# Three maxima slots per item ahead of the attention, and a ScalarE copy of the denominators in layer 1

## The chip, the core and the metric

The kernel runs on one core of a Trainium2 chip. The metric is the device time of one execution in microseconds (us); for the kernel before it is the median of three runs. The core has TensorE (PE, the matmul engine), VectorE (DVE), ScalarE (ACT), GpSimd (POOL) and SyncE (SP, which here only issues transfers). Each runs its own list of instructions in order and waits on semaphores for the others. Matmul results land in PSUM, which PE writes and DVE and ACT read[...].

## What is computed

Two layers on x of shape (2, 256, 64, 64), so two batches of N = 4096 positions. Layer 0 is an attention with 8 heads of width 32, layer 1 a non-local block with a pooled softmax.

```python
# layer 0
q, k, v = split(w_qkv @ x)                      # 8 heads, d = 32, n = 4096
attn = softmax(q^T k / sqrt(d))                 # rows of 4096
x = w_proj @ (attn v) + x
# layer 1
g     = maxpool2(g_w @ x + g_b)                 # 256 x 1024
theta = theta_w @ x[:, :64] + theta_b           # 64 x 4096
phi   = maxpool2(phi_w @ x[:, 64:] + phi_b)     # 64 x 1024
y = softmax(theta^T phi) g                      # rows of 1024
x = batchnorm(W_w @ y + W_b) + x
```

Both softmaxes subtract the maximum of a row before the exponential, so each needs the maxima first, and divides by the sum of a row (the denominator) at the end.

## The kernel before

**Layer 0.** The 8 heads of a batch are two groups of four ("quads"), so there are four units of work, each with 8 blocks of 512 queries. For a block, the attention loop goes over 32 pieces of 128 keys: scores, exponentials on ACT, products with v, sums of the exponentials on POOL. The row maxima of a block have to be there before its attention starts. A generator, `maxes`, yields after each small step of the maxima, in the order of the blocks; `advance(maxes, n)` takes n steps. During the attention two steps stand in each of the 32 rounds, so that the maxima run `LEAD` = 4 rounds and one block ahead.

**Ahead of the attention** there is nothing to hide the first block's maxima, so they run next to the first projections. This front part is issued from the last lines of `conv_attention` (L840 to L853). An *item* is `make("k", 0, i)`, `make("q", 0, i)` or `make("v", 0, i)`: one projection of 512 positions, two matmuls of 128x512 for k and q, eight of 128x128 for v, into a PSUM tile of the pool `ps_m`, and an ACT copy out of it (L211, L194). The first block's maxima come from `first_block` as 33 *slots*. A slot has four matmuls, one for each head (L293), on four different groups of 32 rows of PE, so that they run beside each other. Heads 0 and 1 write into two tiles of `ps_m`, heads 2 and 3 into the two halves of one tile of `ps_s`. The maximum over a pair of key blocks a and b is found as max(b - a, 0) + a: in one slot a head has the product with the key difference, which ACT passes through Relu (L358), in its next slot the product with a itself, which DVE adds to it and reduces (`joint`, L320). Heads 2 and 3 are one slot behind heads 0 and 1, so every full slot has two Relus and two joints. In even slots the joints are those of heads 2 and 3, in odd slots those of heads 0 and 1.

**Buffers.** `ps_m` has four tiles of one bank (`scratch`), which in the front part are given out in turn; `ps_s` has two tiles of two banks (`scores`). An item takes one scratch, a slot two scratches and one scores tile. The next owner of a tile waits for the ACT or DVE instruction that read it last.

**Order of the front before:** k0, k1, q0; then k2 to k7, v0 and v1, with four slots behind each; the last slot; q1; then for each of v2 to v7 one step of the second block's maxima ahead of it (a *step* has two matmuls, for two heads, each followed by a DVE reduction at L305, or by Relu and joint); two more steps. `make_rows()` stands behind v3 and v5; its second call puts the first block's maxima through PE (L150) as rows and copies them (L161), which the attention needs.

**Layer 1.** `non_local` goes over 8 blocks i of 512 positions, in four steps t each: scores (`f2`, L805), exponentials on ACT (L820), and, one step late, `weigh`: four matmuls of 128x512 (L771) into two accumulators `acc[i]` in scratch tiles, while POOL adds the exponentials into `sums` (L763, L767). In between stands one step of `maxima1`: two matmuls (L739) into a scores tile and a DVE reduction (L746). When a block's last `weigh` is issued, `result(i)` follows: a matmul with ones gives the denominators in a scratch tile `den` (L783), DVE takes their reciprocal into `r` in SBUF (L785), two pairs of DVE instructions make z (L787, L790), and SP stores it (L793). Two of the next block's accumulators are then taken from the tiles that come free.

Of the kernel before, what the change touches and what calls it, by code (L numbers as in the profile page):

```python
# [25 lines left out]
NI = N // NB  # L26
# [9 lines left out]
def conv_attention(  # L36
# [13 lines left out]
    nc = tc.nc  # L50
# [20 lines left out]
    def scratch(name):  # L71
        return ps_m.tile([P, NB], F32, tag="m", name=name)
# [3 lines left out]
    def single(name):  # L76
        return probs.tile([P, 2, NB], F32, tag="one", name=name, bufs=ONES)
# [9 lines left out]
    def load_x(b, i, t):  # L87
        nc.sync.dma_start(
            out=t, in_=x[b].rearrange("(o p) n -> p o n", p=P)[:, :, bass.ts(i, NB)]
        )  # L90
        return t
# [76 lines left out]
    q, k, v, kd = {}, {}, {}, {}  # L168
    held = {}

    def make(what, n, i):
        b, qd = QUAD[n]
        if (b, i) not in held:
            name = f"x_{what}_{n}_{i}"
            held.clear()
            held[b, i] = load_x(b, i, xs.tile([P, NC, NB], F32, tag="x", name=name))
        xc = held[b, i]
        name = f"{what}_{b}_{qd}_{i}"
        pq = scratch(name)
        if what == "v":  # L180
            if i == 0:
                v[n] = qkv.tile([P, NJ, QH, D], F32, tag="v", name=f"v_{n}")
            for j in range(NB // P):
                for c in range(NC):
                    nc.tensor.matmul(  # L185
                        pq[:, bass.ts(j, P)],
                        xc[:, c, bass.ts(j, P)],
                        wv_sb[:, c, bass.ts(qd, P)],
                        start=(c == 0),
                        stop=(c == NC - 1),  # L190
                    )
                if j % 2 == 1:
                    yield
            nc.scalar.copy(v[n][:, bass.ts(i, NB // P)].rearrange("p j h d -> p (j h d)"), pq)  # L194
            return
        for c in range(NC):
            nc.tensor.matmul(  # L197
                pq,
                wqk_sb[:, c, qd, 0 if what == "q" else 1, :],
                xc[:, c, :],  # L200
                start=(c == 0),
                stop=(c == NC - 1),
            )
            yield
        if what == "q":
            to = q[n, i] = qkv.tile([P, NB], F32, tag="q", name=f"q_{n}_{i}", bufs=3)
        else:
            if i == 0:
                k[n] = qkv.tile([P, N], F32, tag="k", name=f"k_{n}")
            to = k[n][:, bass.ts(i, NB)]  # L210
        nc.scalar.copy(to, pq)  # L211
        if what == "k" and i % 2 == 0 and i > 0 and n == 0:
            between(n, i // 2 - 1)
        if what == "k" and i == NI - 1 and n == 0:
            rounds(n)
        if what == "k" and i % 2 == 1 and n == 0:
            if i == 1:
                kd[n] = qkv.tile([P, NI // 4, NB], F32, tag="kd", name=f"kd_{n}")
            differences(n, i // 2, (kd[n] if i < NI // 2 else last_kd)[:, i // 2 % (NI // 4), :])
# [5 lines left out]
    def differences(n, c, to):  # L225
        two = k[n][:, bass.ts(c, 2 * NB)]
        nc.gpsimd.tensor_sub(to, two[:, NB:], two[:, :NB])
# [6 lines left out]
    def between(n, c):  # L234
        two = k[n][:, NB * (2 * c + 1) : NB * (2 * c + 3)]
        nc.gpsimd.tensor_sub(mid_kd[:, c, :], two[:, NB:], two[:, :NB])

    def rounds(n):
        nc.gpsimd.tensor_sub(
            turn_kd,  # L240
            k[n][:, P:NB].rearrange("p (a n) -> p a n", n=P),
            k[n][:, N - NB : N - P].rearrange("p (a n) -> p a n", n=P),
        )
# [117 lines left out]
    G = NB // P  # L361
# [38 lines left out]
    def all_maxima():  # L400
        for n in range(len(QUAD)):
            for i in range(NI):
                yield from maxima(n, i)

    maxes = all_maxima()

    def advance(steps, n=1):
        for _ in range(n):
            next(steps, None)
# [3 lines left out]
    def make_rows():  # L413

        for i, r in enumerate(rows):
            if callable(r):
                if i in seen:
                    rows[i] = r()
                seen.add(i)
# [233 lines left out]
    def non_local(b, y, theta_w, phi_w):  # L653
# [125 lines left out]
        def result(i):  # L779
            cols = bass.ts(i, NB)  # L780
            z = single(f"z_{b}_{i}")
            den = scratch(f"den1_{b}_{i}")
            nc.tensor.matmul(den, ones, acc[i][NC], start=True, stop=True)  # L783
            r = work.tile([P, NB], F32, tag="r", name=f"r1_{b}_{i}", bufs=1)
            nc.vector.reciprocal(r, den)  # L785
            for o in range(NC):
                nc.vector.scalar_tensor_tensor(  # L787
                    z[:, o, :], acc[i][o], bn_scale[:, o : o + 1], r, ALU.mult, ALU.mult
                )
                nc.vector.scalar_tensor_tensor(  # L790
                    z[:, o, :], z[:, o, :], bn_shift[:, o : o + 1], y[:, o, cols], ALU.add, ALU.add
                )
            nc.sync.dma_start(out=dst[:, :, cols], in_=z)  # L793
# [3 lines left out]
        for i in range(NI):  # L797
            rows = later
            for t in range(last + 1):
                if t == 0:  # L800
                    s = scores(f"f2_{b}_{i}")
                for h in range(2):
                    half = bass.ts(h, CM)
                    keys = phi if t == 0 else dphi[:, 2 * P * (t - 1) :]
                    nc.tensor.matmul(  # L805
                        s[:, h, :],
                        keys[half, bass.ts(h, P)],
                        theta[i][half, :],
                        start=(t == 0),
                        stop=(t > 0),  # L810
                        skip_group_check=t > 0,
                    )
                for h in range(2):
                    half = bass.ts(h, CM)
                    if t == 0:
                        nc.tensor.matmul(
                            s[:, h, :], ones_b[half, :], rows[half, :], start=False, stop=True
                        )
                p = single(f"p1_{b}_{i}_{t}")
                nc.scalar.activation(p, s, AF.Exp)  # L820
                if waiting is not None:
                    weigh(*waiting)
                waiting = (i, t, p)
                if finish:
                    result(finish.pop())
                if t == last and i + 1 < NI:
                    later = ready[i + 1]()
                advance(maxes1)
        weigh(*waiting)
        result(finish.pop())  # L830


    LEAD = 4
# [6 lines left out]
        held[0, i] = load_x(0, i, x0[:, :, bass.ts(i, NB)])  # L840
    for what, i in (("k", 0), ("k", 1), ("q", 0)):
        advance(make(what, 0, i), 3)
    for what, i in [("k", i) for i in range(2, NI)] + [("v", 0), ("v", 1)]:
        advance(make(what, 0, i), 3)
        advance(maxes, G)
    advance(maxes)
    advance(make("q", 0, 1), 3)
    for i in range(2, NI):
        advance(maxes)
        advance(make("v", 0, i), 3)  # L850
        if i in (3, 5):
            make_rows()
    advance(maxes, 2 * LEAD - NI + 2)  # L853
    held.clear()
    for b in range(B):
        y = big.tile([P, NC, N], F32, tag="y", name=f"y{b}")
# [58 lines left out]
```

## Time and profile before

| what | us |
|---|---|
| median of three runs (3903.01 to 3907.87) | 3904.28 |
| the profiled execution | 3908.37 |
| its span, first to last instruction | 3906.6 |
| PE busy | 3864.0 |
| POOL busy | 3091.5 |
| DVE busy | 2900.7 |
| ACT busy | 2697.5 |
| front part, start of k2 to the attention's first matmul | 14.92 to 96.56 |
| layer 1, first batch, first exponential to the end of the last reciprocal | 1833.1 to 2023.1 |

Busy time of PE is pipelined and its ends are modelled, so a PE that is busy all the time may still be waiting for small amounts; how far apart the starts of equal pieces of work lie says more. PE's granted clock was 0.997 over the span. In the tables of the prediction a row of the timeline reads: start, length, engine, line, operation, what it writes and reads, and in brackets the idle time of its engine before it and what ended that. A row of the chain of waits reads: start, length, what the end of the program was waiting for at that time.

### The profile page before, as it was taken

How to read it: one execution, taken by the hardware profiler on the slowest of the kernel's cores; microseconds unless marked ns; L12 is line 12 of the kernel's file. 1: busy time of each engine (PE TensorE's matmuls, PEld its weight loads, DVE VectorE, ACT ScalarE, POOL GpSimd, SP SyncE). 2: the span in 40 equal slices, each digit the busy share in tenths (PEclk: the TensorE clock that was granted, in tenths of full speed). 3: DMA queues.
4: the chain of work that ended last, by engine and by line, in shares of the span. 5: the costliest groups of instructions: out<-in, count | busy, mean ns of one | idle time of the engine just before them, and what ended most of it. 6: DMA issues, size and time to landing. Idle time of an engine off the chain costs nothing.

```text
span 3906.6 us, 69965 instructions
## 1 busy us (share of the span) xinstructions
PE 3864.0 (99%) x27452; PEld 1366.8 (35%) x27452; DVE 2900.7 (74%) x5449; ACT 2697.5 (69%) x3378; POOL 3091.5 (79%) x1957
## 2 busy tenths in 40 slices
PE   9999999999999999999999999999999999999998
PEld 4333333333333333333333333333333333332333
DVE  5888888788888888764458888888888888884444
ACT  5787777777777777751137777777778888887111
POOL 1888899899989999871448899998999999997043
PEclk9999999999999999999999999999999999999999
DMA  1778878778878788780018888887788888889100
GB/s 57 145 167 169 172 166 170 168 162 172 168 167 169 166 168 169 167 188 6 22 34 169 168 175 168 173 171 164 163 176 171 170 170 170 168 168 188 53 17 27
DMA packets 112300, 566.26 MB, mean 145 GB/s; under 512 B 20200, under 2 KB 22504, under 8 KB 50784
## 3 DMA queue, kind: packets, MB, share of 16 engines
q0 software_dynamic: 68832, 501.25, 63.5%
q1 hardware_dynamic: 42448, 59.74, 4.5%
q8 instruction: 215, 3.52, 0.3%
q14 instruction: 117, 0.96, 0.1%
q10 hardware_dynamic: 688, 0.79, 0.1%
HBM read 51.63 MB, written 8.88 MB: 15 GB/s over the span
## 4 chain that ended last, share of the span: by engine, by line
PE 96%; DVE 2%; DMA 1%; POOL 1%; issue 0%; ACT 0%; DVEq 0%; POOLq 0%; ACTq 0%; SPq 0%
PE s L452 28%; PE w L476 26%; PE ps L293 23%; PE y L771 6%; PE q L197 2%; PE k L197 2%; PE v L185 2%; PE proj L639 1%; PE g L696 1%; DVE r L785 1%; PE f L739 1%; PE f L805 1%; PE den L536 1%; DMA p<-p 1%; PE tp L680 0%; PE tp L676 0%
## 5 line engine op out<-in xcount | busy, mean ns | idle before, releaser
L509 POOL TENSOR_TENSOR p<-p,p 128x1024 f32<-128x1024 f32 x945 | 2364.4, 2502 | 281.4 <-ACT p L598 262.7
L598 ACT ACTIVATE p<-s 128x1024 f32<-128x1024 f32 x2048 | 2087.6, 1023 | 560.5 <-PE ps L293 495.1
L293 PE MATMUL ps<-k,q 32*128 32x512 f32 x6142 | 2020.6, 626 | 2.5 <-DVE r L785 1.3
L305 DVE TENSOR_REDUCE part<-ps 128x1 f32<-128x512 f32 x2046 | 1315.7, 686 | 566.8 <-PE ps L293 563.1
L476 PE MATMUL w<-p,v 128*32 128x512 f32 x8192 | 1091.0, 605 | 1.1 <-ACT p L598 1.1
L452 PE MATMUL s<-q,mid_kd 32*128 32x512 f32 x3072 | 771.2, 615 | 0.0
L320 DVE CUSTOM_DVE_ANT_0 ps<-ps,over 128x512 f32<-128x512 f32 x1025 | 706.2, 691 | 24.9 <-PE ps L293 10.5
L491 DVE TENSOR_TENSOR y<-y,w 128x512 f32<-128x512 f32 x961 | 659.1, 686 | 51.9 <-PE w L476 49.3
L293 PEld LDWEIGHTS ps<-k,q 32*128 32x128 f32 x6142 | 625.1, 183 | 25.6 <-DVE part L320 10.4
L313 ACT ACTIVATE over<-ps 128x512 f32<-128x512 f32 x961 | 569.3, 592 | 10.7 <-PE ps L293 7.9
L293 PE MATMUL ps<-kd,q 32*128 32x512 f32 x1056 | 525.9, 593 | 0.0
L452 PE MATMUL s<-q,last_kd 32*128 32x512 f32 x2048 | 508.5, 615 | 4.5 <-ACT p L598 4.5
L452 PE MATMUL s<-q,kd 32*128 32x512 f32 x2048 | 510.5, 616 | 0.4 <-ACT p L598 0.3
L293 PE MATMUL ps<-last_kd,q 32*128 32x512 f32 x904 | 445.1, 590 | 0.0
L476 PEld LDWEIGHTS w<-p,v 128*32 128x32 f32 x8192 | 161.6, 108 | 805.3 <-DVE part L305 775.2
L452 PEld LDWEIGHTS s<-q,mid_kd 32*128 32x128 f32 x3072 | 270.4, 183 | 443.5 <-ACT over L313 253.9
L515 POOL DMA_DIRECT2D p<-p x448 | 395.3, 882 | 27.3 <-ACT p L598 27.1
L452 PEld LDWEIGHTS s<-q,kd 32*128 32x128 f32 x2048 | 174.0, 184 | 299.8 <-ACT over L313 182.7
L452 PEld LDWEIGHTS s<-q,last_kd 32*128 32x128 f32 x2048 | 172.8, 183 | 284.9 <-ACT over L313 178.5
L771 PE MATMUL y<-p,kv 128*128 128x512 f32 x512 | 240.1, 608 | 6.4 <-DVE r L785 6.4
L820 ACT ACTIVATE p<-f 128x1024 f32<-128x1024 f32 x64 | 65.5, 1023 | 248.5 <-PE f L805 219.2
L767 POOL TENSOR_TENSOR sums<-sums,p 128x512 f32<-128x512 f32 x96 | 121.3, 1264 | 113.7 <-ACT p L820 109.9
(120 smaller groups left out, 2806.3 us busy)
## 6 DMA issues: line engine op xcount, KB each, us to landing
p<-p POOLq DMA_DIRECT2D x478, 1024.0 KB, 7.6
x_q<-in_x_dram SPq DMA_DIRECT2D x30, 512.0 KB
x_k<-in_x_dram SPq DMA_DIRECT2D x24, 512.0 KB
x_res<-in_x_dram SPq DMA_DIRECT2D x16, 512.0 KB
out_dram<-z SPq DMA_DIRECT2D x16, 512.0 KB
r<-flat SPq DMA_DIRECT2D x120, 64.0 KB
x<-in_x_dram SPq DMA_DIRECT2D x8, 512.0 KB
wqk_sb<-in_wqk_dram ACTq DMA_DIRECT2D x1, 512.0 KB
```

Of the source, the lines that this page charges most:

```text
L197: nc.tensor.matmul(pq, wqk_sb[:, c, qd, 0 if what == "q" else 1, :], xc[:, c, :], start=(c == 0), stop=(c == NC - 1),)
L293: nc.tensor.matmul(ps, q[n, i][bass.ts(h, D), bass.ts(g, P)], keys[bass.ts(h, D), :], start=True, stop=True,)
L305: reduced = nc.vector.tensor_reduce(part[:, g, h, j : j + 1], ps, AX.X, ALU.max)
L313: cut = nc.scalar.activation(over, ps, AF.Relu)
L320: reduced = nc.vector.tensor_tensor_reduce(out=ps, in0=ps, in1=over, scale=1.0, scalar=LEAST, op0=ALU.add, op1=ALU.max, accum_out=part[:, ...
L452: nc.tensor.matmul(s[:, t, :], kj[bass.ts(h, D), :], q[blk.n, blk.i][bass.ts(h, D), :], start=False, stop=True, skip_group_check=j > 0,)
L476: nc.tensor.matmul(w[bass.ts(h, D), :], v[blk.n][:, keys(j), h, :], p[h // 2][:, h % 2, :], start=True, stop=True,)
L491: nc.vector.tensor_add(blk.num, blk.num, w)
L509: added = nc.gpsimd.tensor_add(blk.sums[0], blk.sums[0], p[0])
L515: sent = nc.gpsimd.dma_start(out=blk.sums[n], in_=two, accum_op=ALU.add)
L598: nc.scalar.activation(p[pair], s, AF.Exp, scale=scale)
L771: nc.tensor.matmul(acc[i][o], wg[:, 2 * t + j, bass.ts(o, P)], p[:, j, :], **edge)
```

## The change

There are two parts.

- In the front part only three slots stand behind an item, and all of k2 to k7 and v0 to v4 (11 items) have slots behind them: 33 slots. Then q1 follows. v5, v6 and v7 have one step each ahead of them, and five steps follow v7, with `make_rows()` behind the first and behind the third of them. The numbers of items (k, q, v), slots (33) and steps (8) are the same as before.
- In `result(i)` of layer 1, for all blocks but the last, ACT copies `den` from its PSUM tile into `r`, and DVE takes the reciprocal of `r` in place.

```diff
             den = scratch(f"den1_{b}_{i}")
             nc.tensor.matmul(den, ones, acc[i][NC], start=True, stop=True)
             r = work.tile([P, NB], F32, tag="r", name=f"r1_{b}_{i}", bufs=1)
+            if i < NI - 1:
+
+                nc.scalar.copy(r, den)
+                den = r
             nc.vector.reciprocal(r, den)
```

```diff
-    for what, i in [("k", i) for i in range(2, NI)] + [("v", 0), ("v", 1)]:
-        advance(make(what, 0, i), 3)
-        advance(maxes, G)
+    slots = 2 * G * (NI // 2) + 1
+    for n, (what, i) in enumerate([("k", i) for i in range(2, NI)] + [("v", i) for i in range(NI)]):
+        if slots > 0:
+            advance(make(what, 0, i), 3)
+            advance(maxes, min(3, slots))
+            slots -= 3
+            if slots <= 0:
+                advance(make("q", 0, 1), 3)
+        else:
+            advance(maxes)
+            advance(make(what, 0, i), 3)
     advance(maxes)
-    advance(make("q", 0, 1), 3)
-    for i in range(2, NI):
-        advance(maxes)
-        advance(make("v", 0, i), 3)
-        if i in (3, 5):
-            make_rows()
-    advance(maxes, 2 * LEAD - NI + 2)
+    make_rows()
+    advance(maxes, 2)
+    make_rows()
+    advance(maxes, 2 * LEAD - 6)
```

The instructions of POOL and of SP, and their waits, are the same in both programs. On ACT 14 copies are added. In layer 1 the first matmul of each next block's second accumulator, which waited for DVE, waits for ACT; before the last block of both batches, the four matmuls of its first `weigh` go in turn between the two accumulators where before both of the first came ahead of both of the second, and in the first batch a small matmul of the coming attention (L464), which stood among them, goes behind the last denominators' matmul.

## The prediction

> **What bounds the kernel now.** I read the page first (busy times and the chain that ended last), then the chain of waits through the front part, the timeline of one period there, and the timeline of layer 1 around one `result`, with the row of the reciprocal for who waits for it.
>
> ```profile
> PE 3864.0 (99%) x27452; PEld 1366.8 (35%) x27452; DVE 2900.7 (74%) x5449; ACT 2697.5 (69%) x3378; POOL 3091.5 (79%) x1957
> PE 96%; DVE 2%; DMA 1%; POOL 1%; issue 0%; ACT 0%; DVEq 0%; POOLq 0%; ACTq 0%; SPq 0%
> ```
>
> PE is on 96% of the chain. Time goes only where PE gets less to do or waits less; a shorter DVE or ACT counts only where PE waits for it. The 2% of DVE are such places, and the reciprocal at L785 (1% of the chain by the page) is the largest.
>
> Chain of waits, front part (start, length, what):
>
> ```profile
> 28.64 1.91 PE k L197 x4
> 30.56 5.43 PE ps L293 x31
> 35.99 1.92 PE k L197 x4
> 37.91 5.43 PE ps L293 x31
> ...
> 74.53 1.93 PE q L197 x4
> ...
> 95.65 1.79 PE ps L293 x8
> ```
>
> A period is one item and four slots, 7.35 us. It reads as pure PE, but four slots take 5.43 where two full slots follow each other after 0.97 when nothing holds them (30.49 and 31.46 below), so 3.9 would do. The timeline of that period shows what holds them:
>
> ```profile
> 30.49 0.70 PE L293 MATMUL ps<-kd,q 32*128 32x512 f32 x2
> 31.65 3.04 ACT L358 ACTIVATE over<-ps 128x512 f32<-128x512 f32 x6 [0.47 <-PE ps L293]
> 31.85 0.70 DVE L320 CUSTOM_DVE_ANT_0 ps<-ps,over 128x512 f32<-128x512 f32 x1 [1.40 <-ACT k L211]
> 32.75 0.70 DVE L320 CUSTOM_DVE_ANT_0 ps<-ps,over 128x512 f32<-128x512 f32 x1
> 33.36 0.73 DVE L320 CUSTOM_DVE_ANT_0 ps<-ps,over 128x512 f32<-128x512 f32 x1
> 33.56 1.99 PE L293 MATMUL ps<-k,q 32*128 32x512 f32 x7
> 34.01 0.73 DVE L320 CUSTOM_DVE_ANT_0 ps<-ps,over 128x512 f32<-128x512 f32 x1
> ```
>
> The third slot's heads 2 and 3 start at 33.56, when the joint of 32.75 has left their scores tile (its end with the accumulator's read is 33.51). DVE starts 1.40 late, since it drained while PE ran the item. So PE and DVE wait for each other in turn.
>
> Layer 1, timeline around one `result`:
>
> ```profile
> 1855.88 1.02 PE L783 MATMUL den<-sums,ones 128*128 128x512 f32 x2
> 1856.84 1.13 PE L739 MATMUL f<-kv,theta 64*128 64x512 f32 x4
> 1856.94 3.36 DVE L785 RECIPROCAL r<-den 128x512 f32<-128x512 f32 x1 [4.33 <-PE den L783]
> 1858.75 1.13 PE L771 MATMUL y<-p,kv 128*128 128x512 f32 x2
> 1860.22 1.16 DVE L746 TENSOR_REDUCE neg<-f 128x1 f32<-128x1024 f32 x1
> 1860.36 2.84 PE L771 MATMUL y<-p,kv 128*128 128x512 f32 x6 [0.47 <-DVE r L785]
> 1863.13 1.13 PE L739 MATMUL f<-kv,theta 64*128 64x512 f32 x4
> 1868.68 1.13 PE L739 MATMUL f<-kv,theta 64*128 64x512 f32 x4
> ```
>
> The next block's second accumulator takes the bank of `den`, which DVE reads for 3.36 us; PE waits for it at 1860.36. A step with this wait takes 6.29 us (1856.84 to 1863.13), the next, of the same matmuls, 5.55.
>
> [...]
>
> **The change, layer 1.** It adds an ACT copy of 128x512 from PSUM, 14 times, at 0.58 us (the copies at L211 have that length). ACT is idle there: its next instruction after 1856.91, when `den` ends, is the exponential at 1858.93. So the copy runs at 1856.95 to 1857.53, delays nothing queued behind it, and frees the bank 2.2 us before PE wants it (about 1859.71). DVE's reciprocal starts at 1857.57 in place of 1856.94. That its source is SBUF should cost nothing: the same operation at the end of layer 0, on r in place, took 3.36 (1755.43 to 1758.78).
>
> What is late next on DVE is the reduction L746 behind the reciprocal, at 1860.85 to 1862.01 in place of 1860.22 to 1861.38. It frees the scores tile of the next matmul on f, which without the stall comes at 1863.13 - 0.74 = 1862.39: 0.38 us of slack, less the 0.05 or so of a semaphore. Then z ends 0.6 later against an unchanged rest; POOL and SP have several us before `sums`, z or r are needed again. The gain is 6.29 - 5.55 = 0.74 for blocks 0 to 5 of both batches, 12 x 0.74 = 8.9. For block 6, in the second batch PE went from 3879.84 to 3880.91 (1.07) where 0.43 is the pitch, with a restart of 0.54 for 0.43: 0.7. In the first batch a small matmul of the attention lay in that gap and now stands elsewhere: 0.3. Sum 9.9 us. Below: if the slack is gone in all steps, some 0.3 each is lost, 4 us. Above nothing: these are all the stalls.
>
> **The change, front part.** No instruction is added or removed; the x blocks have landed before (the DMA view of the first 60 us has no traffic between 19 and 27 us), and POOL's key differences of 1.27 us are ready a slot or more early. So the price is how long a period of an item and three slots takes, and how many there are. I carry the rules of the trace through it by hand, with time 0 at an item's end:
> - slot A starts at 0, its matmuls end at 1.13; B follows at 0.97. ACT's Relus of A are over at 1.75 and 2.24 (pitch 0.48).
> - DVE begins 0.23 after A's matmuls, at 1.36. If A is even, its two joints share a scores tile and start 0.90 apart, 1.51 for both; odd, 0.65 apart, 1.30. A tile is free 0.79 after its joint's start.
> - C's heads 0 and 1 start at 1.84 and 2.29, after A's Relus; heads 2 and 3 at 3.07, after A's second joint (2.26 + 0.79).
> - In the four-slot period D waits for B's joints (3.52 + 0.79 = 4.31), starts its last at 4.37, and 1.06 later the next item starts: 5.43, which is the 5.43 of the chain. The rules fit.
>
> With three slots the item starts 1.05 after C: at 4.12. Its own bank (B's first joint) is free at 3.66. Period even-odd-even: 4.12 + 1.92 = 6.04. Odd-even-odd: A's joints start at 1.36 and 2.01, the middle slot's at 2.66 and 3.56; C's heads 0 and 1 wait for A's joints, 2.15 and 2.80 plus 0.06, the item starts at 2.86 + 1.04 = 3.90, period 5.82. Mean 5.93, or 1.98 us a slot against 1.84 before, with three more items done on the way. From k2 on: the first three slots find DVE's queue empty (first joint at 18.70), so that by the same rules k3 starts near 19.9 and ends at 21.85. Then five periods of 5.82 and four of 6.04, and 0.06 more for each of five v: 53.6, to 75.4. The last three slots take 4.1: q1 at 79.5, 5.0 later than before, with v2 to v4 done. The tail before, from q1 (74.53) to the end of v7 (95.65), is 21.1; without three steps with their v (3.04 each) it is 12.0: v7 ends at 91.5. Five steps follow instead of two. With four banks, a DVE reduction of 0.65 per head and the small transposes among them they take about 5.5 in place of 4.8 unheld; two took 1.95. So the attention's flow begins at 97.0 in place of 97.6: 0.6 us gained, DVE about 1 us further behind, which the attention takes up (DVE is busy 82.6 us of the stretch from 400 to 500). Several roundings of 0.1 in ten periods: between 3 lost and 4 gained.
>
> **Sum.** 9.9 + 0.6 = 10.5. The profiled execution took 3908.37 (span 3906.6 and 1.8 around it), 4.1 above the median; its stalls are counts of waits that every execution has, so the same 10.5 is taken from the median: 3904.28 - 10.5 = 3893.8.
>
> **The rivals.**
> - *The front runs at PE's pace.* If DVE's backlog drains beside the items, three slots take 2.9 and a period 4.85: some 10.8 more, 3883. For it: DVE's need of 4.2 per period is under 4.85. Against it: the rules that give 5.43 have PE wait for A's joints, whatever stands behind C.
> - *The layer 1 gain is half taken back.* The later reduction L746 holds the next matmul on f, or the copy comes late behind another ACT wait: 3898 to 3900. For it: only 0.3 us of slack. Against: ACT is idle, and the slack is positive.
> - *The front loses 3 to 5.* Each period 0.3 to 0.5 longer than worked out: 3897 to 3899.
> - *Slower: full drain.* The item takes its bank from a joint in every other period. If PE could start it only after DVE had emptied all three slots, a period would be 1.92 + 1.36 + 4.32 + 0.2 = 7.8, ten of them 18.7 us more than mine: 3912. It decides from a period of 7.0 on, where the ten cost what all else gains. Against it: the bank is that of the middle slot, free at 3.66.
>
> **How the numbers follow.** Forecast 0.70, with a range of its own of 3890 to 3897; PE's pace 0.10; half taken back 0.08; front loses 0.08; full drain 0.04. About 0.2% (7.8 us, 3896.5) is what a measurement of this kernel tells from no change. Of the forecast's 0.70, some 0.03 lie beyond it. Faster: 0.67 + 0.10 = 0.77; within: 0.03 + 0.16 = 0.19; slower: 0.04. The range of 3886 to 3899 holds the forecast and the two rivals that lose a little, and leaves out most of PE's pace and the full drain.
>
> **What would show it.** After the change the wait of PE's y for r should be gone, the step with `result` should take 5.55, and the reduction behind the reciprocal should end before the next matmul on f. In the front the chain should show an item every 5.8 and 6.0 in turn, q1 near 79.5, and the first L464 within 1.5 us of 96.56. Periods near 4.9 or above 7, or a step with `result` above 6, would make it wrong.

## The result, and the profile after

The changed kernel takes 3893.77 us (median of six runs, 3891.81 to 3896.36), the kernel before 3906.07 (six runs, 3903.01 to 3912.77, the three of the prediction among them). The ratio is 0.997, with a 95% interval of 0.996 to 0.998: faster by 12.3 us, or 0.3%. The profiled execution took 3891.81 us, with a span of 3890.0, 16.6 under the span of before; part of that belongs to the two executions and not to the change, as the table below shows.

Page of the changed kernel, busy times and the chain by engine:

```profile
PE 3854.8 (99%) x27452; PEld 1362.5 (35%) x27452; DVE 2903.0 (75%) x5449; ACT 2705.7 (70%) x3392; POOL 3091.2 (79%) x1957
PE 96%; DMA 2%; POOL 1%; DVE 1%; issue 1%; ACT 0%; DVEq 0%; POOLq 0%; ACTq 0%; SPq 0%
```

ACT has 14 instructions and 8.2 us more, DVE as many instructions as before. DVE's share of the chain went from 2% to 1%: 14 of the 16 reciprocals are no longer on it. Timeline of the changed kernel around the first `result` of layer 1 (the copy is L787, the reciprocal L789):

```profile
1852.93 1.02 PE L783 MATMUL den<-sums,ones 128*128 128x512 f32 x2
1853.88 1.13 PE L739 MATMUL f<-kv,theta 64*128 64x512 f32 x4
1853.99 0.58 ACT L787 COPY r<-den 128x512 f32<-128x512 f32 x1 [3.46 <-PE den L783]
1854.61 3.35 DVE L789 RECIPROCAL r<-r 128x512 f32<-128x512 f32 x1 [4.95 <-ACT r L787]
1855.80 3.70 PE L771 MATMUL y<-p,kv 128*128 128x512 f32 x8
1857.88 1.16 DVE L746 TENSOR_REDUCE neg<-f 128x1 f32<-128x1024 f32 x1
1859.43 1.13 PE L739 MATMUL f<-kv,theta 64*128 64x512 f32 x4
1864.98 1.13 PE L739 MATMUL f<-kv,theta 64*128 64x512 f32 x4
```

All eight matmuls on y now run through (x8 with no idle time in brackets, where before it was x2, a gap, x6). The step with the result takes 1859.43 - 1853.88 = 5.55 us, as the next one does (1864.98 - 1859.43); before it was 6.29. The rows of the reciprocal show both sources, SBUF (`r`) and PSUM (`den`), next to each other. Reading from SBUF had no price here, 3353 ns in the median against 3358:

```profile
L789 DVE RECIPROCAL r<-r x14: 3352/3353/3354, 1854.6 to 3862.4; 128x512 f32<-128x512 f32 x14
L789 DVE RECIPROCAL r<-den x2: 3358/3358/3358, 2011.6 to 3880.2; 128x512 f32<-128x512 f32 x2
```

Chain of waits in the front part of the changed kernel (start, length, what):

```profile
24.15 1.91 PE k L197 x4
26.06 4.13 PE ps L293 x24
30.19 1.91 PE k L197 x4
32.10 1.17 PE ps L293 x8
...
35.90 1.91 PE k L197 x4
37.81 4.13 PE ps L293 x23
41.94 1.91 PE k L197 x4
...
77.52 1.93 PE q L197 x4
```

Items start 6.04 and 5.71 us apart in turn (24.15, 30.19, 35.90, 41.94). q1 starts 64.2 us after k2 (k2's row in this chain is at 13.36; the instruction itself starts at 13.20), where before it was 59.6, with three more items done.

The places where the two profiled executions differ, from the starts of the same instructions in both traces. "First w" is the attention's first product with v (L476); layer 1 is from the first to the eighth matmul on `den` of a batch:

| stretch | before, us | after, us | gained |
|---|---|---|---|
| span's start to k2 | 14.75 | 13.20 | 1.55 |
| k2 to the attention's first w | 88.10 | 86.80 | 1.30 |
| from there to the first den, first batch | 1753.03 | 1752.93 | 0.10 |
| layer 1, first batch | 162.80 | 157.59 | 5.21 |
| eighth den to the second batch's first w | 11.32 | 10.17 | 1.15 |
| from there to its first den | 1702.75 | 1700.84 | 1.91 |
| layer 1, second batch | 162.80 | 157.59 | 5.21 |
| from its eighth den to the end | 11.02 | 10.90 | 0.12 |

Only the second and the two layer-1 rows, 11.7 us, have a cause in the changed instructions. The others come up under the front order alone: they differ about as much between kernels that are the same there.

### The profile page after: what moved, and what is told of

The parts are those of the page before. It is cut to its first block, busy times and chain, and to the rows that moved or that the text cites. A ratio compares the mean times of both kernels' runs of the same rounds, so it can differ in the third digit from the quotient of the medians.

```text
span 3890.0 us, 69990 instructions
## 1 busy us (share of the span) xinstructions
PE 3854.8 (99%) x27452; PEld 1362.5 (35%) x27452; DVE 2903.0 (75%) x5449; ACT 2705.7 (70%) x3392; POOL 3091.2 (79%) x1957
## 4 chain that ended last, share of the span: by engine, by line
PE 96%; DMA 2%; POOL 1%; DVE 1%; issue 1%; ACT 0%; DVEq 0%; POOLq 0%; ACTq 0%; SPq 0%
PE s L452 27%; PE w L476 26%; PE ps L293 23%; PE y L771 6%; PE q L197 2%; PE f L739 2%; PE k L197 2%; PE v L185 2%; PE proj L639 1%; PE f L809 1%; PE g L696 1%; DMA p<-p 1%; PE den L536 1%; PE tp L680 0%; PE tp L676 0%
## 5 line engine op out<-in xcount | busy, mean ns | idle before, releaser
L476 PE MATMUL w<-p,v 128*32 128x512 f32 x8192 | 1091.0, 605 | 1.1 <-ACT p L598 1.1
L293 PEld LDWEIGHTS ps<-k,q 32*128 32x128 f32 x6142 | 622.6, 183 | 27.7 <-DVE part L320 12.4
L476 PEld LDWEIGHTS w<-p,v 128*32 128x32 f32 x8192 | 161.1, 108 | 805.1 <-DVE part L305 775.0
```

The costliest lines, as they stand in the source:

```text
L293: nc.tensor.matmul(ps, q[n, i][bass.ts(h, D), bass.ts(g, P)], keys[bass.ts(h, D), :], start=True, stop=True,)
L476: nc.tensor.matmul(w[bass.ts(h, D), :], v[blk.n][:, keys(j), h, :], p[h // 2][:, h % 2, :], start=True, stop=True,)
```

## The experiments

All were timed against the kernel before on the chip that they ran on, and each profile was cut into the stretches of the table above. A ratio and its interval are estimates from the single runs; a ratio can differ from the quotient of the two medians in the fourth decimal.

### The copy alone

The front part is that of before. (A bank, in what follows, is the PSUM space of one 128x512 fp32 tile of the pool `ps_m`.)

```diff
             den = scratch(f"den1_{b}_{i}")
             nc.tensor.matmul(den, ones, acc[i][NC], start=True, stop=True)
             r = work.tile([P, NB], F32, tag="r", name=f"r1_{b}_{i}", bufs=1)
+            if i < NI - 1:
+                nc.scalar.copy(r, den)
+                den = r
             nc.vector.reciprocal(r, den)
```

> The kernel before with the ScalarE copy of the denominators alone. Theory (the early release of the bank of den makes nearly all of the gain): each of the 14 steps with a result takes 5.55 us in place of 6.29, 10.4 in sum, and about 1 more at the start of the second batch's attention, where PE's order changed: 11 us under the kernel before, 3895 where before is 3906. Rival (the front part gave a third or more): 7 to 8 us under before.

Measured: 3895.09 us, ratio 0.9965 (0.9953 to 0.9978), 13.0 under before. Layer 1 takes 157.59 us in both batches, the number of the changed kernel; k2 to the first w takes 88.09, the number of before. The copy is the gain that a measurement can tell. The 10.4 us of its two layer-1 stretches lie inside the interval; the rest of the 13.0 is not assigned.

### The front order alone

```diff
-            if i < NI - 1:
-
-                nc.scalar.copy(r, den)
-                den = r
             nc.vector.reciprocal(r, den)
```

(against the changed kernel)

> The kernel before with the new front order alone. Theory: periods of 6.04 and 5.7 to 5.8 in turn, the attention's first rounds (first w) 1.3 us earlier counted from the start of k2, so 1 to 1.5 us under the kernel before, not to be told from no change. Rival (the front is worth what the profile shows in all, 2.85 at the attention's first w): 3 us under before, with k2 again 1.5 earlier. Second rival (the front costs, and the copy hides it): slower than before.

Measured: 3905.99 us against 3908.05, ratio 0.9997 (0.9989 to 1.0005): no change that can be told. k2 to the first w takes 86.79, so the 1.30 us are the new order's and no more; layer 1 is 162.80. Three other rows of the table can be judged from this profile and its neighbours.

The start of k2 is one. It is at 14.11 here, and in the eleven profiles of this document between 13.20 and 14.75, with the same instructions ahead of it. The first of them, the matmuls of k0 and k1, start alike but do not last alike. Timeline of the kernel before, then of the changed kernel:

```profile
6.68 6.52 PE L197 MATMUL k<-x,wqk_sb 128*128 128x512 f32 x8 [6.68 <-DMA wqk_sb<-in_wqk_dram]
6.50 5.14 PE L197 MATMUL k<-x,wqk_sb 128*128 128x512 f32 x8 [6.50 <-DMA wqk_sb<-in_wqk_dram]
```

That is 1.38 of the 1.55 us. The traces' records of the granted clock begin at full speed, at 12.4 us in the kernel before and at 9.4 in the changed one; ahead of that there is no record, but in the kernel before the two matmuls of k1 start 1.71 us apart and those of k2 0.86. Counted by single instructions, the starts lie 0.85 to 0.86 us apart up to 11.96 us in the kernel before and up to 9.23 in the changed one (but for the first two, 1.01 and 1.02), and 0.43 apart from 12.61 and 9.77 on. So in both the pace changes where the record begins, and this row goes with the time at which the single execution comes to the faster pace. That the clock makes it is an estimate from these starts, since no record covers the slow stretch.

The second is the stretch from the eighth den to the second batch's first w. It takes 10.52 here, although this kernel's layer 1 is that of before, where it took 11.32. In the copy alone, of which about 1 us was expected there, it takes 10.17, and in the changed kernel 10.17 in one profile and 10.38 in another. So 0.80 of the 1.15 is there without the copy, and the 0.35 left is little more than the 0.21 by which two profiles of one kernel differ. The third is the stretch from there to the next den, which in all eleven profiles lies between 1700.8 and 1706.0. So the 1.55, most of the 1.15 and the 1.91 of the table are not the change's.

### VectorE makes the copy

```diff
             if i < NI - 1:
 
-                nc.scalar.copy(r, den)
+                nc.vector.tensor_copy(r, den)
                 den = r
```

> The changed kernel with the copy of den made by VectorE in place of ScalarE. Theory (what counts is that the bank is free before PE wants it, 2.8 us after den ends): the copy takes 0.6 to 0.7 of DVE, the bank is free as early, steps with a result stay at 5.55 to 5.65, the time is that of the changed kernel within 1.5 us. Rival (the gain hangs on ScalarE doing it, since VectorE's list gets longer ahead of the reduction that frees the scores tile): steps of 5.8 or more, 3 us or more above the changed kernel.

Measured: 3896.39 us, ratio 0.9968 (0.9956 to 0.9981). Layer 1 takes 157.91 and 157.59. Timeline of this kernel at the first result:

```profile
1855.74 1.13 PE L739 MATMUL f<-kv,theta 64*128 64x512 f32 x4
1855.85 0.69 DVE L787 COPY r<-den 128x512 f32<-128x512 f32 x1 [4.33 <-PE den L783]
1856.58 3.35 DVE L789 RECIPROCAL r<-r 128x512 f32<-128x512 f32 x1
1857.66 3.70 PE L771 MATMUL y<-p,kv 128*128 128x512 f32 x8
1859.85 1.16 DVE L746 TENSOR_REDUCE neg<-f 128x1 f32<-128x1024 f32 x1
1861.29 1.13 PE L739 MATMUL f<-kv,theta 64*128 64x512 f32 x4
```

The step stays at 5.55, and the time is 11.7 us under the kernel before, where the changed kernel was 12.3 under it. So the engine of the copy does not matter, and the gain does not come from less work on DVE, which here has more of it: the bank's early release is what counts. The reduction ends at 1861.01, 0.28 ahead of the next matmul on f.

### The slack behind the reciprocal

Two more VectorE copies of `r` in place stand ahead of the reciprocal.

```diff
                 nc.scalar.copy(r, den)
                 den = r
+                nc.vector.tensor_copy(r, r)
+                nc.vector.tensor_copy(r, r)
             nc.vector.reciprocal(r, den)
```

> The changed kernel with two more VectorE copies of r in place between ScalarE's copy and the reciprocal, 14 times. Theory (the reduction behind the reciprocal ends 0.39 us before PE's next matmul on f needs its scores tile): the copies put some 0.6 to 0.8 on DVE, the slack is gone, and a step with a result takes 0.2 to 0.4 more than 5.55: 2.5 to 5 us above the changed kernel. Rival (that tile is not what comes next, so DVE has more room): steps stay at 5.55.

Measured: 3907.10 us against 3908.12, ratio 0.9995 (0.9987 to 1.0004): no gain over the kernel before that a measurement can tell is left. Timeline at the first result:

```profile
1855.52 1.13 PE L739 MATMUL f<-kv,theta 64*128 64x512 f32 x4
1856.24 0.43 DVE L789 COPY r<-r 128x512 f32<-128x512 f32 x1 [4.95 <-ACT r L787]
1857.17 3.35 DVE L791 RECIPROCAL r<-r 128x512 f32<-128x512 f32 x1
1860.44 1.16 DVE L746 TENSOR_REDUCE neg<-f 128x1 f32<-128x1024 f32 x1
1861.65 1.13 PE L739 MATMUL f<-kv,theta 64*128 64x512 f32 x4 [0.52 <-DVE neg L746]
```

The two copies put the reciprocal 1.58 us behind `den` in place of 0.66. PE now waits 0.52 us for the reduction, and the step takes 1861.65 - 1855.52 = 6.13. This is 0.92 more on DVE, less 0.39 of slack, and some 0.05 until PE starts again: 0.58 a step, above the 0.2 to 0.4 expected, because the copies took 0.92 and not 0.6 to 0.8. Layer 1 takes 162.29 and 161.11, 8.2 us more than in the changed kernel, where 2.5 to 5 was expected. That is still less than the loss in the medians: the version below, timed beside it on the same chip, has the changed kernel's 157.59 twice and took 3896.86, 10.2 less. Another 0.8 us stands in the stretch from the eighth den to the second batch's first w (11.54 against 10.76). In it PE's granted clock is half for 10.2 us from 2021.7, where that version has 3.4 from 2018.2; further on each of the two has one more piece of 3.4 (mean granted clock of the two profiles: 0.997 and 0.998). Whether the clock makes this loss, and what the rest is, was not tried apart.

### The copy for the last block of the first batch as well

```diff
-            if i < NI - 1:
+            if i < NI - 1 or b < B - 1:
 
                 nc.scalar.copy(r, den)
```

> The changed kernel with the copy of den for the first batch's last block too. Theory (PE's gap of 1.32 us at the second batch's attention, ended by the reciprocal at the release of den's bank, is the same stall as the other 14): the gap goes, the half clock behind it too, 1.5 to 3 us less. Rival (DVE is in the reciprocal all the same, so that the reductions of the attention's maxima, which free the other banks, come no earlier): PE stands still one matmul later, and the time is that of the changed kernel within 1 us.

Measured: 3896.86 us, ratio 0.9971 (0.9961 to 0.9982). Timeline at the start of the second batch's attention:

```profile
2013.60 3.35 DVE L789 RECIPROCAL r<-r 128x512 f32<-128x512 f32 x1 [12.08 <-ACT r L787]
2016.87 0.63 DVE L305 TENSOR_REDUCE part<-ps 128x1 f32<-128x512 f32 x1
2017.55 1.48 PE L293 MATMUL ps<-kd,q 32*128 32x512 f32 x2 [2.48 <-DVE part L305]
```

PE's gap is 2.48 us and not 0: with den's bank free PE runs one more matmul, and then needs a bank that only the reduction behind the reciprocal frees. The stretch to the first w is 10.76 us against 10.17 and 10.38 in the changed kernel's two profiles, and the ratio to the kernel before is the changed kernel's (0.997). The rival holds: here the bank freed early did not help, because another one was held behind the same instruction a moment later.

### Two slots per item

15 items (q1 among them) with two slots behind each, then the last three slots and eight steps.

```diff
-    slots = 2 * G * (NI // 2) + 1
...
+    for what, i in [("k", i) for i in range(2, NI)] + [("v", i) for i in range(NI - 1)] + [("q", 1), ("v", NI - 1)]:
+        advance(make(what, 0, i), 3)
+        advance(maxes, 2)
+    advance(maxes, 3)
     advance(maxes)
     make_rows()
-    advance(maxes, 2)
+    advance(maxes, 4)
     make_rows()
-    advance(maxes, 2 * LEAD - 6)
+    advance(maxes, 2 * LEAD - 5)
```

> The changed kernel with two slots behind each of 15 items (k2 to k7, v0 to v6, q1, v7), then three slots and eight steps. Theory (PE waits only from the third slot on, whose heads 2 and 3 need the scores tile that the first slot's joints hold): an item and two slots take 1.92 + 2.03 = 3.95 us in each period, PE runs without a wait, and the attention starts some 7 us earlier than in the changed kernel: 3886 to 3887 where it takes 3893.8. Rival (the period is set by the round trip from matmul to joint to matmul, whatever the number of slots, or DVE's backlog is only moved to the end): periods of 4.6 or more, or a wait of 4 us or more in the last slots and steps; 3891 to 3895.

Measured: 3892.29 us, ratio 0.9960 (0.9947 to 0.9974); k2 to the first w 82.44, which is 4.4 less than in the changed kernel where 7 were expected. Chain of waits of this kernel, then what the stretches from 60 us on show (stretch; its length, busy time of PE, PEld, DVE, ACT and POOL with their instructions; granted clock, DMA share, GB/s):

```profile
33.25 1.91 PE k L197 x4
35.16 1.93 PE ps L293 x16
37.09 1.98 PE v L185 x16
39.07 1.93 PE ps L293 x16
41.00 1.98 PE v L185 x16
```

```profile
60.00:73.00 13.00, 13.00 (x95) 7.68 (x88) 9.63 (x27) 9.29 (x19) 0.00 (x0) 1.00 0.00 1
73.00:83.00 10.00, 7.76 (x38) 3.16 (x36) 9.47 (x25) 3.70 (x7) 1.22 (x5) 1.00 0.00 1
83.00:93.20 10.20, 10.20 (x38) 6.12 (x38) 5.78 (x12) 2.28 (x4) 0.00 (x0) 0.50 0.01 2
```

The periods are as expected: 1.93 for two slots, 3.84 to 3.91 with the item. So it is the third slot that holds PE. The time was not as expected: 3886 to 3887 was forecast, and 3892.29 lies in the rival's range. The second half of the rival, DVE's backlog moved to the end, is what the rows show. From 73 to 83 us DVE is busy for 9.47 of 10 with ten joints, most of them of the five slots that stand in a row behind v7, and five reductions of the steps; PE is busy for 7.76, and then its granted clock is 0.50 for 10.2 us.

### Eight slots first

k2 is followed by the eight slots that need only k0 and k1; then two behind each item; the last slot and the steps have v6 and v7 among them.

```diff
+    advance(make("k", 0, 2), 3)
+    advance(maxes, 8)
+    for what, i in [("k", i) for i in range(3, NI)] + [("v", i) for i in range(5)] + [("q", 1), ("v", 5)]:
+        advance(make(what, 0, i), 3)
+        advance(maxes, 2)
+    advance(make("v", 0, 6), 3)
+    advance(maxes, 2)
+    advance(make("v", 0, 7), 3)
     make_rows()
-    advance(maxes, 2)
+    advance(maxes, 5)
     make_rows()
     advance(maxes, 2 * LEAD - 6)
```

(in place of the changed kernel's loop over items and the `advance(maxes)` behind it)

> The changed kernel with eight slots behind k2 (they need k0 and k1 alone), then two behind each of k3 to k7, v0 to v4, q1 and v5, one behind v6, and v7 between the first two of the eight steps. Theory (what held the two-slot version back was DVE's backlog in its last three slots, behind which PE stood still and its granted clock fell to half for 10.2 us at 83 us): without slots in a row at the end PE has no such gap, the clock stays at 1.0 in the front, the attention's first w comes some 8 us earlier than in the changed kernel counted from the start of k2, and the time is 8 us under it: 3886. Rival (the clock falls for another reason[...]): a fall in the front again and 3890 or more.

Measured: 3890.29 us, ratio 0.9955 (0.9942 to 0.9967); k2 to the first w 79.82, 7.0 less than in the changed kernel. The same stretch as above in this kernel:

```profile
73.00:83.00 10.00, 10.00 (x67) 6.11 (x67) 7.13 (x19) 4.49 (x9) 1.22 (x5) 1.00 0.00 1
83.00:93.20 10.20, 9.84 (x58) 3.95 (x57) 8.47 (x18) 5.51 (x8) 0.00 (x0) 1.00 0.01 2
```

The clock stays at 1.00 in this execution. Of the 2.6 us between the two versions' fronts, how much is the clock and how much DVE's backlog was not tried apart. Nor does one profile speak for all executions. The profiled one is the fastest of five (3886.82), and three of the others have a mean granted clock of 0.996, the figure of all five executions of the two-slot version, against 0.998 in the profiled one; where they lost it is not recorded. The median is 4 us above the 3886 expected, in the range of the rival, so that a fall of the clock in this front is not ruled out. One us of the eight expected in the front is missing in the profile too, and the chain says where:

```profile
26.22 1.93 PE k L197 x4
28.17 0.59 ACT k L211
28.83 1.27 POOL kd L227
30.15 1.99 PE ps L293 x12
```

The slots after k3 need the difference of k3 and k2, and wait for ACT's copy and POOL's subtraction.

### Six slots first

The same with `advance(maxes, 6)` behind k2, and two slots behind v6.

> The version with eight slots behind k2, with six there in place of eight, and two more behind v6. Theory (PE's 2 us at 28 us are slot 9's wait for the key difference of k2 and k3, which ScalarE's copy of k3 and GpSimd's subtraction of 1.27 us make): with k3 two slots earlier that wait is hidden, the attention's first w comes 2 us earlier than in the version with eight, counted from the start of k2 (77.8 where that took 79.8, and the changed kernel 86.8), and the time is 8 to 9 us under the changed kernel of the same chip. Rival (the wait comes back elsewhere in the front, or the clock falls): 79 or more to the first w, 7 us or less under the changed kernel.

Measured: 3887.07 us (3885.20 to 3888.88), ratio 0.9945 (0.9933 to 0.9958), the lowest of all versions here, though its interval overlaps that of the eight-slot version; k2 to the first w 77.83, as expected. The wait for the key difference is gone from the chain:

```profile
15.65 7.70 PE ps L293 x41
23.34 1.91 PE k L197 x4
25.26 1.93 PE ps L293 x16
27.19 1.91 PE k L197 x4
```

One wait is left in this front: PE stands still for 1.07 us ahead of the last slot, at 74.85 (the changed kernel has it too, at 76.39). Behind v6 three slots follow each other again; the version with eight slots has one there, and no such wait.

### The changed kernel again, on that chip

> The changed kernel once more, beside the version above on the same chip. Expected 10 to 13 us under the kernel before, with 14 steps of 5.55 us and 86.8 us from the start of k2 to the first w, as in its first profile; what differs between its profiles (the start of k2, the length of the half clock behind PE's gaps) belongs to the single run.

Measured: 3895.15 us against 3907.95, ratio 0.9969 (0.9957 to 0.9981); k2 to the first w 86.80, layer 1 157.59 twice. The six-slot version is 8.1 us under it, and 8 to 9 was expected.

## Why the prediction was right

3893.8 was forecast and 3893.77 measured. That the two agree to the tenth is chance. The gain was 12.3 us, where the sum said 10.5, and the median of the kernel before came out 1.8 higher with six runs (3906.07) than with the three from which the forecast started (3904.28); the two differences cancel. Timed once more, the changed kernel took 3895.15, with a gain of 12.8. The stretches of the traces that the change accounts for sum to 11.7. Step by step:

- **What bounds the kernel.** PE's chain, with the reciprocal as the largest place where it waits. Shown by the copy alone: 13.0 us, against 2.1 (not to be told from nothing) for the front alone.
- **Layer 1, sum 9.9.** Measured 2 x 5.21 = 10.4 in the traces. The 12 steps at 0.74 came out to the hundredth. The term that was mis-sized is block 6 of the first batch, taken at 0.3 and measured at 0.74: the small matmul of the attention that had stood in that gap takes nothing off the gain, and no cost of it shows where it went.
- **The copy's cover and the slack.** The copy was put at 0.58 us on an idle ACT, and is that. The reduction was to end 0.38 us ahead of PE's next matmul on f, and ends 0.39 ahead (1859.04 and 1859.43). That this is what comes next was argued then; the two added copies showed it, where PE waits for exactly that reduction.
- **Reciprocal from SBUF at no cost.** 3353 ns against 3358.
- **The front, 0.6.** The periods were worked out at 6.04 and 5.82 and came out at 6.04 and 5.71; q1 was to start 64.6 us after k2 and does after 64.2. The attention's first matmul (L464) starts 81.19 us after k2 in place of 81.81, which is the 0.6 of the sum. At the first w the gain is 1.3: the second L464, which started 0.73 us behind the first, now starts 0.05 behind it, and the working had no term for that. The sign "within 1.5 us of 96.56" was missed, at 94.39, because k2 itself started 1.55 earlier in this execution. The rules carried by hand also gave the reason, that C's heads 2 and 3 wait for A's joints; with two slots per item there is no such slot, and the period is 1.91 + 1.93.
- **The rivals.** "PE's pace" did not come for three slots per item, and does come for two. "Half taken back" needs 0.4 us more on DVE than there is; the two added copies bring it. The front did not lose, and the full drain did not come.
- **Not in the working.** The profiled span fell by 16.6, 4.9 more than the changed stretches account for. The prediction took both executions to be alike outside the change, which profiles here are not, by 1 to 5 us in a stretch; medians of several runs even out part of that.

## What to carry to other kernels

A slow instruction that reads a PSUM bank (here the reciprocal, 3358 ns against 742 for the first DVE instruction of z on as many elements) is worth a copy ahead of it (here 0.58 us) when the bank, and not its result, is what PE waits for (0.74 us a step here); before counting the gain, look for the next instruction behind the slow one that frees something PE needs (here 0.39 us away), and at the one place here where it held two banks at once the copy did nothing. Where work for PE alone is mixed with slots that make a round trip over DVE, count how many slots fit into the buffers before the first one has to come back: here two did, so that two per item and not three or four let PE run through. Of the three versions with two slots per item, the ones with the remaining slots in a row at the start, where DVE has no backlog, had a shorter front (79.8 and 77.8 us) than the one with them at the end (82.4).

## What the runs showed of the hardware that was not expected

No profile has the full clock over its span: the means of the granted clock are 0.996 to 0.998. In the kernel before, it is half for 6.83 us from 1732.71, for 6.83 from 2022.84 and for the last 8.44 from 3900.17; in the changed kernel for 6.83 from 1729.76, for 3.41 from 2016.48 and for the last 8.48 from 3883.57; in the front of the version with two slots per item for 10.2. So the pieces ahead of the last have lengths of 3.4, 6.8 and 10.2. The longest gap of PE in each of these two goes with one of them: PE stands still at the end of the first batch's attention for 4.81 us in the kernel before (to 1734.85) and for 4.80 in the changed kernel (to 1731.88), and the 6.83 us at half clock begin within that gap. But shorter gaps also go with a half clock here. In the kernel before, PE's gap of 1.32 us at the start of the second batch's attention ends at 2023.15 and 6.8 us at half clock begin at 2022.8; in the changed kernel the same gap ends at 2014.99 and 3.4 us at half clock begin at 2016.5 (the granted clock is the number after the five busy times):

```profile
2022.80:2029.60 6.80, 6.45 (x24) 4.05 (x24) 6.03 (x11) 2.64 (x3) 0.00 (x0) 0.50 0.20 77
```

```profile
2016.50:2019.90 3.40, 3.40 (x17) 2.13 (x15) 2.99 (x7) 1.77 (x3) 0.00 (x0) 0.50 0.26 102
```

The stretch from the eighth den to the first w took 11.32 us with 6.8 us at half clock. The kernel with the new front order alone, whose instructions there are those of before, took 10.52 with 3.4 (mean granted clock of its profile 0.998, of the kernel before 0.997). So 3.4 us more at half clock went with 0.8 us more time. Nor is every such gap followed by a half clock: a gap of 1.59 us in the kernel before (it ends at 2862.62) and one of 1.50 us in the changed kernel (at 2853.19) have a granted clock of 1.00 behind them. The stretch behind the first:

```profile
2862.60:2873.00 10.40, 10.38 (x80) 3.36 (x80) 7.08 (x13) 8.41 (x12) 10.40 (x7) 1.00 0.61 126
```

What decides between the two cases was not tried.
